# Splitting the FFN's layer norm between VectorE and ScalarE, moving the last image's ReLUs, and setting the times of all steps anew

## The chip, the cores and the metric

The kernel runs on one core of one Trainium2 chip. The metric is the device time in microseconds of one execution. Engines are called as in the profile: PE is TensorE's matmul, PEld its weight load, DVE is VectorE, ACT is ScalarE, POOL is GpSimd, SP is SyncE, which here only issues DMAs.

## The reference

Thirty-two images of 56 x 56 positions and 96 channels go through two layers.

```python
# layer 0: layer norm over channels, a product to 192 channels, a 3x3 convolution back to 96, silu, residual
h = (x - mu) * rsqrt(var + eps) * ln_w + ln_b
x1, z = split(einsum('bhwc,cd->bhwd', h, w_in) + b_in)
x = x + silu(conv3x3(x1, conv_w) + conv_b)
# layer 1, mixing: norm, product to 192, batch norm and relu, FFT over the 3136 positions,
# a diagonal complex product with relu on both parts, inverse FFT, product back to 96, batch norm
t = t + attn(_ln_t(t))
# layer 1, FFN: norm, product to 384 and relu, product back to 96;
# operands are rounded to an 8-bit float (5 exponent, 2 mantissa bits), sums to 16 bits
t = t + ffn(_ln_t(t))
```

`_ln_t` takes the mean and the variance over the 96 channels of a position and gives (t − mean) / sqrt(var + 1e-5). z is not used.

## The kernel before, in words

Each image passes four stages, which overlap with those of other images: at any time the convolution of one image, the first half of the mixing of the image before, the second half of the mixing of the one before that and the FFN of a still earlier one are under way. A tile of tokens has 112 partitions (positions) and 28 columns of positions; a group is four of these columns, so an image has 7 groups. The norm's statistics are taken in 4 chunks of two groups (the last has one).

The work is cut into steps. A step is a small Python function of one image, and `put(when, f, ...)` gives it a time; the unit is one eighth of an image's period, so steps of image b stand at 8 b + when. All steps of all images are sorted by these times and recorded in that order. A scheduler then sets the order of each engine's instructions from the recorded program by its own simulated times, so the order on an engine follows the times roughly, not exactly. Tiles come from pools in rotation. PSUM has four such rotations of two buffers each: "a" (the transposed tokens tp_n and the FFN's first product pf), "q" (im, cv, st of the convolution), "b" (pa, pg, pe, po) and "c" (ph, px, py).

The names that the text uses, in the order in which an image meets them:

- `fetch` (the DMA is issued in a helper, L356) loads a chunk xl of the image for the first norm, into one of three buffers; `take_in` takes its statistics (st_a, on DVE, L141; var_a, L145; rs_a = var to the power −1/2 on POOL, L147) and makes xa (DVE, L409). `make_image` multiplies xa on PE into im (L165), and ACT copies it into img (L167). `load` brings the same tokens a second time, into t, for the residual.
- `conv_part` is the convolution cv (L180, L184), three parts in each of three rounds; ACT and DVE make m, sd and s of it, `conv_tokens` turns s back into tokens st (PE, L216), and DVE adds them to t (L438).
- `norm_b` takes the statistics of the second norm (st_b, var_b, rs_b); `tokens_a` transposes a group into tp_n (PE, L158), and ACT copies it to n2t (L222). `forth` is the product ph (PE, L229), with a ReLU into h on ACT (L232); `forth_a` is the first transform pa (PE, L238), copied to u on ACT (L239); `store_a` writes u to da in HBM.
- `fetch_a` reads da back in another layout into at; `second` is the second transform px (PE, L253), from which ACT and DVE make av, sv and gt; `second_w2` is the product pg (PE, L296), gw its copy; `second_back` the first inverse transform pe (PE, L306), es its copy; `store_back` writes es to de in HBM.
- `fetch_y` reads de back into y, one of four buffers; `back` is the last inverse transform py (PE, L314); `back_end` adds it to t on DVE (L515) and takes the statistics of the FFN's norm (st_c, var_c, rs_c).
- `normal` (L520) makes the FFN's norm xn of a group in two calls of two columns each, all on DVE (L529); `ffn_start` transposes xn into tp_n (PE, L156) and copies it to n3t (ACT). `ffn_first` is pf (PE, L325) with the copy h1 on ACT (L327), three times per group; `ffn_middle` adds the bias and takes the ReLU into h2 and rounds it to hq (DVE, L335 and L336). In the last image two of the three ReLUs of a group are on ACT (L333). `ffn_second` is po (PE, L342), with the copy y1 on ACT (L346); `ffn_end` adds the bias and the residual (DVE, L351 and L352), and `store` writes the group of t to the result (`out`).

All loads and stores inside the loop are issued by SP, one queue in program order: one that has to wait holds up those behind it. `plan` (L558) holds the times of all steps; `CONV`, `FIRST`, `BACK` and `FFN` are the times at which the convolution, the first transform, the last transform and the FFN of an image begin, `S0` and `SS` the start and the spacing of the second transform's units. The last image and the two before it have corrections of their own.

Of the kernel before, what the change touches and what calls it, by code (L numbers as in the profile page):

```python
# [38 lines left out]
F32 = mybir.dt.float32  # L39
F16 = mybir.dt.float16  # L40
F8 = mybir.dt.float8e5
AF = mybir.ActivationFunctionType
ALU = mybir.AluOpType
AX = mybir.AxisListType

C = 96
HW = 56
N = HW * HW
N1, N2 = 112, 28
# [36 lines left out]
def hybrid_kernel(ctx: ExitStack, tc: tile.TileContext, x, par, spar, cpar, w_in, conv_w, w1, w2, fw1, fb1, fw2, fb2, fa, fb, ib, ia, rows6, out):  # L86
    nc = tc.nc
    nb = x.shape[0]
# [27 lines left out]
    b1q = const.tile([128, 3], F32, name="b1q")  # L116
# [13 lines left out]
    stp = ctx.enter_context(tc.tile_pool(name="stp", bufs=3))  # L130
# [198 lines left out]

    def ffn_relu(h1, hq, b, g, k):  # L330
        h2 = w3.tile([128, G4 * N1], F16, tag="h2", name=f"h2_{b}_{g}_{k}")
        if b == nb - 1 and k:
            nc.scalar.activation(h2, h1, AF.Relu, bias=b1q[:, k : k + 1])  # L333
        else:
            nc.vector.tensor_scalar(h2, h1, b1q[:, k : k + 1], 0.0, ALU.add, ALU.max)  # L335
        nc.vector.tensor_copy(hq[:, k, :], h2, saturate=False)  # L336

    def ffn_out(hq, b, g):
# [21 lines left out]
    class Image:  # L360


        def __init__(self, b):
            self.b = b
            self.tokens = x[b].rearrange("(p j) c -> p j c", j=N2)
            self.result = out[b].rearrange("(p j) c -> p j c", j=N2)
            self.t, self.s, self.n2t, self.hq = {}, {}, {}, {}
            self.u, self.at, self.gt, self.gw, self.held = {}, {}, {}, {}, {}
            self.xa, self.xc, self.rs, self.xl, self.y, self.norm = {}, {}, {}, {}, {}, {}

        def hold(self, half):
            n = G4 * (HALVES[half][1] - HALVES[half][0])
            self.t[half] = tpool.tile([N1, n, C + 1], F32, tag=f"t{half}", name=f"t_{self.b}_{half}")
# [146 lines left out]
    def normal(im, g, j):  # L520

        i = g // 2
        if j == 0:
            im.xc[g] = xnp.tile([N1, G4, C], F8, tag="xn", bufs=2, name=f"xn_{im.b}_{g}")
        mu, _, rs = im.norm[i]
        xc = im.xc[g]
        for j in (j, j + 1):
            at = g % 2 * G4 + j
            nc.vector.tensor_scalar(xc[:, j], im.chunk(i)[:, at, :C], mu[:, at : at + 1], rs[:, at : at + 1], ALU.subtract, ALU.mult, saturate=False)  # L529

    def ffn_start(im, g):
        im.held["n3", g] = ffn_tokens(im.xc.pop(g), im.b, g)
# [4 lines left out]
    def ffn_middle(im, g, k):  # L537
        if k == 0:
            im.hq[g] = w3.tile([128, 3, G4 * N1], F8, tag="hq", name=f"hq_{im.b}_{g}")
        ffn_relu(im.held.pop(("h1", g, k)), im.hq[g], im.b, g, k)  # L540
# [17 lines left out]
    def plan(b):  # L558
        im = Image(b)

        def put(when, f, *args):
            order.append((8 * b + when, len(order), lambda: f(im, *args)))

        last = b == nb - 1
        CONV, FIRST, BACK, FFN = ALL
        S0, SS = 0, 2
        if nb - 4 < b < nb - 1:
            BACK, FFN = BACK + 0.762, FFN + 0.3
        if last:

            FIRST, FFN = FIRST - 0.101, FFN - 0.127
            S0 = -0.975
        back_step, ffn_step = (0.763, 0.962) if last else (0.756, 0.962)

        for i, (j0, j1) in enumerate(LN_CHUNKS):
            at = CONV - 2.503 + 0.691 * i
            ahead = 12 if b == 0 else 2.55 - 0.221 * i
            put(CONV - 7.98 + 0.01 * i if b == 1 else at - ahead, fetch, i)
            put(at - 0.55, take_in, i)
            for j in range(0, j1 - j0, 2):  # L580
                put(at + 0.066 * j, make_image, i, j)
            put(CONV + 5.858 + 1.131 * i, norm_b, i)
            put(FIRST + 2 * i - 0.477, deviation, i)
            if b:
                put(CONV - 0.456 + 0.815 * i, load, i)
        put(CONV - 0.183, make_seam)
        for r in range(NR):
            at = CONV + 1.899 * r
            for part, when in enumerate((0, 0.321, 0.817)):
                put(at + when, conv_part, r, part)  # L590
            put(at + 0.72, conv_first, r)
            put(at + 1.356, conv_last, r)
            for half in range(2):
                put(at + 1.757 + 0.239 * half, conv_tokens, r, half)
                put(at + 1.818 + 0.239 * half, conv_end, r, half)
        for g in range(NG):
            at = FIRST + g
            put(at - 0.407, tokens_a, g)
            for j2 in range(2):
                put(at + 0.065 + 0.467 * j2, forth, g, j2)  # L600
                put(at + 0.536 + 0.58 * j2, forth_a, g, j2)
            put(at + 1.249, store_a, g)
            at = BACK + back_step * g
            put(max(S0 + 4 * SS - 0.003, at - 2.9), fetch_y, g)
            put(at, back, g)
            put(at + 0.06, back_end, g)
            at = FFN + ffn_step * g
            put(at - 0.797, normal, g, 0)
            put(at - 0.375, normal, g, 2)
            put(at - 0.365, ffn_start, g)  # L610
            for k in range(3):
                put(at + 0.336 * k, ffn_first, g, k)
                put(at + 0.336 * k + 0.208, ffn_middle, g, k)
            put(at + 0.912, ffn_second, g)
            put(at + 0.997, ffn_end, g)
            put(at + 1.5, store, g)
        for g in range(NS):
            put(max(FIRST + 7.508, S0 + g - (1.4 if g % 2 else 2.2)), fetch_a, g)
        for m, (p0, p1) in enumerate(UNITS):
            both = p1 - p0 > PG  # L620
            for at, u in ((0, 0), (0.606, 1), (1.069, 2)) if both else ((0, 0), (0.674, 2)):
                at += S0 + SS * m + (0.125 if m + u == 0 else 0)
                put(at, second, m, u)
                put(at + 0.22, second_parts, m, u)
                put(at + 0.512, second_relus, m, u)
            for j0 in range(0, (p1 - p0) // 2, 2):
                at = S0 + SS * m + (2.024 if both else 1.3) - 0.017 * j0
                put(at, second_w2, m, j0)
                put(at + 0.2, second_back, m, j0)
                put(at + 0.575, store_back, m, j0)  # L630
# [1 line left out]
    def load(im, i):  # L632
        im.load(i)

    CONV, FIRST, BACK, FFN = -14.872, -8.324, 8.016, 10.65
    ALL = CONV, FIRST, BACK, FFN
    for b in range(nb):
        plan(b)
# [15 lines left out]
    with tc.tile_pool(name="setup", bufs=1) as sp, tc.tile_pool(  # L654
        name="setup_ps", bufs=2, space=bass.MemoryType.PSUM
# [284 lines left out]
```

## Time and profile before

| | |
|---|---|
| time, three runs | 3091.17, 3093.26, 3093.85 us; median 3093.26 |
| the profiled execution | 3090.75 us |
| its span, from the first to the last instruction | 3089.0 us |
| mean granted TensorE clock | 0.986 |
| the clock in the last 96 us | 0.77 |
| PE, DVE, ACT busy from 1351 to 1448 us | 96.4, 79.2 and 69.6 of 97 us |
| DVE: one xn of 96 elements (x896) | 238.5 us together, 325 ns each |
| DVE: one ReLU of 448 elements (x658) | 213.9 us together, 330 ns each |
| ACT: one ReLU of 448 elements (x14) | 9.4 us together, 683 ns each |

A group's busy time counts overlapping instructions once, so it is below the count times the mean duration where they follow one another without a pause. Idle time that the page shows before an instruction belongs to its engine; what ended it is inferred from the semaphores.

### The profile page before, as it was taken

To read this page: it belongs to the slowest core of one execution; us is meant where nothing else is said; L and a number is where in the kernel's file an instruction comes from. 1 tells how busy PE (TensorE), PEld (TensorE's weight loads), DVE (VectorE), ACT (ScalarE), POOL (GpSimd) and SP (SyncE) were. 2 spreads that over 40 slices of the span, in tenths; PEclk is the share of its full clock that TensorE was granted. 3 is DMA by queue.
4 is the path that set the end of the run, shared out by engine and by line. 5 is a ranking of instruction groups with operands and counts; after the bars stand their busy time and mean duration, and the time that the engine had idled before them with its cause. 6 is when DMAs were issued, how large, how long until landed. Compare 5 with 4: busy or idle time off the path is not lost.

```text
span 3089.0 us, 84367 instructions
## 1 busy us (share of the span) xinstructions
PE 3000.8 (97%) x32693; PEld 2446.7 (79%) x32693; DVE 2439.2 (79%) x7554; ACT 2139.5 (69%) x5269; POOL 616.7 (20%) x398
## 2 busy tenths in 40 slices
PE   7899999999999999999999999999999999999998
PEld 5678788888788887788887888887888887788775
DVE  5548787888788888788888788888788887787778
ACT  3456667777667777677776677776677776676776
POOL 2202112222112222112221122221122221122111
PEclk9999999999999999999999999999999999999997
DMA  3532444443444443444443444444444444444442
GB/s 69 148 99 84 122 123 124 115 123 100 122 130 124 114 121 101 120 129 126 112 119 105 120 128 127 114 112 112 120 124 124 120 110 112 120 125 106 114 112 74
DMA packets 495436, 355.37 MB, mean 115 GB/s; under 512 B 329993, under 2 KB 459305, under 8 KB 494809
## 3 DMA queue, kind: packets, MB, share of 16 engines
q1 hardware_dynamic: 493146, 349.24, 42.8%
q8 instruction: 257, 4.21, 0.6%
q14 instruction: 145, 1.18, 0.1%
q10 hardware_dynamic: 1888, 0.74, 0.1%
HBM read 195.73 MB, written 154.14 MB: 113 GB/s over the span
## 4 chain that ended last, share of the span: by engine, by line
PE 88%; DMA 5%; DVE 3%; ACT 2%; issue 1%; SPq 0%; POOL 0%; DVEq 0%; ACTq 0%
PE cv L184 13%; PE ph L229 10%; PE px L253 10%; PE pa L238 9%; PE im L165 8%; PE pe L306 6%; PE pg L296 5%; PE py L314 5%; PE pg L292 5%; PE po L342 4%; PE pf L325 4%; PE cv L180 3%; PE st L216 3%; DMA de<-es 2%; PE tp_n L158 2%; DMA y<-de 2%
## 5 line engine op out<-in xcount | busy, mean ns | idle before, releaser
L184 PE MATMUL cv<-img,wv 97*32 97x196 f32 x13248 | 628.0, 332 | 0.0
L147 POOL TENSOR_TENSOR rs_c<-var_c,mhalf 112x8 f32<-112x8 f32 (+1 forms) x128 | 192.0, 1500 | 1965.0 <-DVE var_b L145 1261.4
L184 PEld LDWEIGHTS cv<-img,wv 97*32 97x32 f32 x13248 | 424.3, 109 | 112.6
L232 ACT ACTIVATE h<-ph,rs_b 112x192 f32<-112x192 f32 x896 | 338.3, 444 | 128.9 <-PE ph L229 127.9
L229 PE MATMUL ph<-w1a,n2t 97*112 97x192 f32 x1792 | 386.7, 338 | 3.3 <-DVE t L515 1.7
L253 PEld LDWEIGHTS px<-fb_sb,at 112*64 112x64 f32 (+1 forms) x3584 | 321.0, 167 | 75.9 <-issue 18.7
L238 PE MATMUL pa<-h,fa_sb 112*112 112x384 f32 x896 | 366.8, 491 | 4.9 <-DVE w1q L799 4.9
L327 ACT CAST h<-pf 128x448 f16<-128x448 f32 x672 | 364.8, 566 | 5.8 <-PE pf L325 3.0
L253 PE MATMUL px<-fb_sb,at 112*64 112x112 f32 (+3 forms) x3584 | 358.4, 274 | 7.4 <-DMA at<-da 3.8
L165 PE MATMUL im<-rows_sb,xa 112*97 112x168 f32 x1792 | 330.7, 310 | 3.1 <-DVE xa L409 1.9
L229 PEld LDWEIGHTS ph<-w1a,n2t 97*112 97x112 f32 x1792 | 273.2, 177 | 55.1 <-issue 15.9
L269 DVE SCALAR_TENSOR_TENSOR sv<-px,spar_sb,av 128x224 f32<-128x224 f32 (+2 forms) x352 | 153.9, 437 | 189.1 <-ACT av L260 188.3
L258 ACT ACTIVATE av<-px,spar_sb 128x224 f32<-128x224 f32 (+2 forms) x352 | 159.8, 454 | 200.5 <-PE px L253 199.6
L239 ACT COPY u<-pa 112x384 f32<-112x384 f32 x448 | 223.2, 498 | 102.9 <-PE pa L238 94.3
L165 PEld LDWEIGHTS im<-rows_sb,xa 112*97 112x97 f32 x1792 | 260.7, 166 | 38.5 <-issue 15.9
L147 POOL TENSOR_TENSOR rs_b<-var_b,mhalf 112x8 f32<-112x8 f32 (+1 forms) x128 | 201.8, 1578 | 425.8 <-DVE var_a L145 344.6
L336 DVE CAST hq<-h 128x448 fp8e5<-128x448 f16 x672 | 255.9, 387 | 10.2 <-ACT h L333 1.9
L335 DVE TENSOR_SCALAR h<-h,b1q 128x448 f16<-128x448 f16 x658 | 213.9, 330 | 58.9 <-ACT h L327 58.4
L141 DVE BATCH_NORM_STATS2 st_a<-xl 112x6 f32<-112x192 f32 x434 | 131.5, 353 | 154.6 <-DMA xl<-in_x 154.6
L296 PE MATMUL pg<-w2x,gt 128*112 128x96 f32 (+1 forms) x1792 | 243.5, 259 | 0.0
L529 DVE TENSOR_SCALAR xn<-t,st_c,rs_c 112x96 fp8e5<-112x96 f32 x896 | 238.5, 325 | 4.8 <-POOL rs_c L147 4.7
L296 PEld LDWEIGHTS pg<-w2x,gt 128*112 128x112 f32 (+1 forms) x1792 | 241.1, 178 | 0.0
(120 smaller groups left out, 6200.7 us busy)
## 6 DMA issues: line engine op xcount, KB each, us to landing
da<-u SPq DMA_DIRECT2D x224, 336.0 KB, 2.9
at<-da SPq DMA_DIRECT2D x224, 336.0 KB, 4.0
de<-es SPq DMA_DIRECT2D x448, 84.0 KB, 2.0
y<-de SPq DMA_DIRECT2D x224, 168.0 KB, 2.6
out<-t SPq DMA_DIRECT2D x224, 168.0 KB, 3.0
t<-in_x SPq DMA_DIRECT2D x96, 336.0 KB, 7.3
xl<-in_x SPq DMA_DIRECT2D x93, 336.0 KB, 4.1
t<-in_x SPq DMA_DIRECT2D x32, 168.0 KB, 4.3
```

The costliest lines, as they stand in the source:

```text
L147: nc.gpsimd.tensor_tensor(rs, var, mhalf[:, :n], ALU.pow)
L165: nc.tensor.matmul(ps[:, j], xa[:, j, :], rows6_sb, start=True, stop=True)
L184: tc.keep_in_program_order(nc.tensor.matmul(*args, start=(dx == 0), stop=(dx == 2)))
L229: nc.tensor.matmul(ph[:, j, :], n2t[:, 2 * j2 + j, :], w1a, start=True, stop=True)
L232: nc.scalar.activation(h[:, j], ph[:, j], AF.Relu, scale=rs[:, 2 * j2 + j : 2 * j2 + j + 1])
L238: nc.tensor.matmul(pa, fa_sb, h, start=True, stop=True)
L239: nc.scalar.copy(u[:, 2 * j2 : 2 * j2 + 2, :], pa)
L253: nc.tensor.matmul(px[rows, j], lhs, fb_sb[:, first(p) : first(p + 1)], start=True, stop=True)
L296: nc.tensor.matmul(pg[:, half, j, :], lhs, w2x, start=False, stop=True, skip_group_check=True)
L327: nc.scalar.copy(h1, pf)
L336: nc.vector.tensor_copy(hq[:, k, :], h2, saturate=False)
L529: nc.vector.tensor_scalar(xc[:, j], im.chunk(i)[:, at, :C], mu[:, at : at + 1], rs[:, at : at + 1], ALU.subtract, ALU.mult, saturate=False)
```

## The change

In `normal`, the first two columns of a group go to ACT, as an activation with the factor rs and the offset −mean · rs, and the last two stay on DVE. The offset, `shift`, is a new small tile, made on DVE once for each chunk. In `ffn_relu` the branch that put two of three ReLUs of the last image on ACT is gone. In `plan` nearly every time has another value, those of the last images too; no step is added or left out. In the diff below, steps of `plan` whose times are given only another value are cut where the text does not speak of them.

```diff
     def ffn_relu(h1, hq, b, g, k):
         h2 = w3.tile([128, G4 * N1], F16, tag="h2", name=f"h2_{b}_{g}_{k}")
-        if b == nb - 1 and k:
-            nc.scalar.activation(h2, h1, AF.Relu, bias=b1q[:, k : k + 1])
-        else:
-            nc.vector.tensor_scalar(h2, h1, b1q[:, k : k + 1], 0.0, ALU.add, ALU.max)
+        nc.vector.tensor_scalar(h2, h1, b1q[:, k : k + 1], 0.0, ALU.add, ALU.max)
         nc.vector.tensor_copy(hq[:, k, :], h2, saturate=False)
...
     def normal(im, g, j):
         i = g // 2
+        mu, _, rs = im.norm[i]
         if j == 0:
             im.xc[g] = xnp.tile([N1, G4, C], F8, tag="xn", bufs=2, name=f"xn_{im.b}_{g}")
-        mu, _, rs = im.norm[i]
+            if g % 2 == 0:
+                im.shift[i] = stp.tile([N1, mu.shape[1]], F32, tag="shift", name=f"shift_{im.b}_{i}")
+                nc.vector.scalar_tensor_tensor(im.shift[i], mu, -1.0, rs, ALU.mult, ALU.mult)
         xc = im.xc[g]
         for j in (j, j + 1):
             at = g % 2 * G4 + j
-            nc.vector.tensor_scalar(xc[:, j], im.chunk(i)[:, at, :C], mu[:, at : at + 1], rs[:, at : at + 1], ALU.subtract, ALU.mult, saturate=False)
+            t, scale = im.chunk(i)[:, at, :C], rs[:, at : at + 1]
+            if j < 2:
+                nc.scalar.activation(
+                    xc[:, j], t, AF.Identity, bias=im.shift[i][:, at : at + 1], scale=scale, saturate=False
+                )
+            else:
+                nc.vector.tensor_scalar(
+                    xc[:, j], t, mu[:, at : at + 1], scale, ALU.subtract, ALU.mult, saturate=False
+                )
...
         if nb - 4 < b < nb - 1:
-            BACK, FFN = BACK + 0.762, FFN + 0.3
+            BACK, FFN = BACK + 0.4, FFN + 0.284
         if last:
-            FIRST, FFN = FIRST - 0.101, FFN - 0.127
-            S0 = -0.975
-        back_step, ffn_step = (0.763, 0.962) if last else (0.756, 0.962)
+            CONV, FIRST, FFN = CONV - 0.074, FIRST - 0.016, FFN - 0.721
+            S0, SS = -0.831, 2.033
+        back_step, ffn_step = (0.82, 0.962) if last else (0.775, 0.971)
         for i, (j0, j1) in enumerate(LN_CHUNKS):
-            at = CONV - 2.503 + 0.691 * i
-            ahead = 12 if b == 0 else 2.55 - 0.221 * i
+            at = CONV - 2.485 + 0.531 * i
+            ahead = 12 if b == 0 else 2.489 - 0.221 * i
             put(CONV - 7.98 + 0.01 * i if b == 1 else at - ahead, fetch, i)
             put(at - 0.55, take_in, i)
...
             at = FFN + ffn_step * g
             put(at - 0.797, normal, g, 0)
-            put(at - 0.375, normal, g, 2)
-            put(at - 0.365, ffn_start, g)
+            put(at - 0.639, normal, g, 2)
+            put(at - 0.329, ffn_start, g)
...
-            put(at + 0.912, ffn_second, g)
-            put(at + 0.997, ffn_end, g)
-            put(at + 1.5, store, g)
+            put(at + 0.96, ffn_second, g)
+            put(at + 0.986, ffn_end, g)
+            put(at + 1.483, store, g)
         for g in range(NS):
-            put(max(FIRST + 7.508, S0 + g - (1.4 if g % 2 else 2.2)), fetch_a, g)
+            put(max(FIRST + 7.433, S0 + g - (1.479 if g % 2 else 1.667)), fetch_a, g)
...
-    CONV, FIRST, BACK, FFN = -14.872, -8.324, 8.016, 10.65
+    CONV, FIRST, BACK, FFN = -15.042, -8.232, 8.036, 10.805
```

More of the change, by code (lines that the diff above doesn't have):

```diff
@@ L369, in __init__ @@
             self.xa, self.xc, self.rs, self.xl, self.y, self.norm = {}, {}, {}, {}, {}, {}
+            self.shift = {}
         def hold(self, half):
@@ L580, in plan @@
             for j in range(0, j1 - j0, 2):
-                put(at + 0.066 * j, make_image, i, j)
-            put(CONV + 5.858 + 1.131 * i, norm_b, i)
+                put(at + 0.08 * j, make_image, i, j)
+            put(CONV + 5.967 + 1.132 * i, norm_b, i)
             put(FIRST + 2 * i - 0.477, deviation, i)
             if b:
-                put(CONV - 0.456 + 0.815 * i, load, i)
-        put(CONV - 0.183, make_seam)
+                put(CONV - 0.346 + 0.78 * i, load, i)
+        put(CONV - 0.078, make_seam)
         for r in range(NR):
-            at = CONV + 1.899 * r
-            for part, when in enumerate((0, 0.321, 0.817)):
+            at = CONV + 1.91 * r
+            for part, when in enumerate((0, 0.139, 0.817)):
                 put(at + when, conv_part, r, part)
             put(at + 0.72, conv_first, r)
-            put(at + 1.356, conv_last, r)
+            put(at + 1.385, conv_last, r)
             for half in range(2):
-                put(at + 1.757 + 0.239 * half, conv_tokens, r, half)
-                put(at + 1.818 + 0.239 * half, conv_end, r, half)
+                put(at + 1.757 + 0.21 * half, conv_tokens, r, half)
+                put(at + 1.858 + 0.21 * half, conv_end, r, half)
         for g in range(NG):
@@ L600, in plan @@
                 put(at + 0.065 + 0.467 * j2, forth, g, j2)
-                put(at + 0.536 + 0.58 * j2, forth_a, g, j2)
-            put(at + 1.249, store_a, g)
+                put(at + 0.536 + 0.659 * j2, forth_a, g, j2)
+            put(at + 1.2, store_a, g)
             at = BACK + back_step * g
-            put(max(S0 + 4 * SS - 0.003, at - 2.9), fetch_y, g)
+            put(max(S0 + 3 * SS + 2 - 0.003, at - 3.004), fetch_y, g)
             put(at, back, g)
-            put(at + 0.06, back_end, g)
+            put(at + 0.113, back_end, g)
             at = FFN + ffn_step * g
             put(at - 0.797, normal, g, 0)
-            put(at - 0.375, normal, g, 2)
-            put(at - 0.365, ffn_start, g)
+            put(at - 0.639, normal, g, 2)
+            put(at - 0.329, ffn_start, g)
             for k in range(3):
@@ L613, in plan @@
                 put(at + 0.336 * k + 0.208, ffn_middle, g, k)
-            put(at + 0.912, ffn_second, g)
-            put(at + 0.997, ffn_end, g)
-            put(at + 1.5, store, g)
+            put(at + 0.96, ffn_second, g)
+            put(at + 0.986, ffn_end, g)
+            put(at + 1.483, store, g)
         for g in range(NS):
-            put(max(FIRST + 7.508, S0 + g - (1.4 if g % 2 else 2.2)), fetch_a, g)
+            put(max(FIRST + 7.433, S0 + g - (1.479 if g % 2 else 1.667)), fetch_a, g)
         for m, (p0, p1) in enumerate(UNITS):
             both = p1 - p0 > PG
-            for at, u in ((0, 0), (0.606, 1), (1.069, 2)) if both else ((0, 0), (0.674, 2)):
+            for at, u in ((0, 0), (0.606, 1), (1.099, 2)) if both else ((0.028, 0), (0.674, 2)):
                 at += S0 + SS * m + (0.125 if m + u == 0 else 0)
@@ L624, in plan @@
                 put(at + 0.22, second_parts, m, u)
-                put(at + 0.512, second_relus, m, u)
+                put(at + 0.47, second_relus, m, u)
             for j0 in range(0, (p1 - p0) // 2, 2):
-                at = S0 + SS * m + (2.024 if both else 1.3) - 0.017 * j0
+                at = S0 + SS * m + (2.024 if both else 1.221) - 0.01 * j0
                 put(at, second_w2, m, j0)
```

## The prediction

> **What bounds the kernel now.** First the page: the span and the busy shares.
>
> ```profile
> span 3089.0 us, 84367 instructions
> PE 3000.8 (97%) x32693; PEld 2446.7 (79%) x32693; DVE 2439.2 (79%) x7554; ACT 2139.5 (69%) x5269; POOL 616.7 (20%) x398
> PE 88%; DMA 5%; DVE 3%; ACT 2%; issue 1%; SPq 0%; POOL 0%; DVEq 0%; ACTq 0%
> ```
>
> TensorE sets the time: 88% of the chain that ended last is its own work. Moving work between VectorE (79%) and ScalarE (69%) gains nothing by itself; only 88 us in which PE has no matmul can be won. The windows by image put some 32 of these before 290 us, 25 after 2895 us, and about 30 in between: a little over 1 us per image. Second, the waits of that middle stretch (300 to 2835 us; columns: total us, times, longest):
>
> ```profile
> DVE st_a L141 <- DMA xl<-in_x: 141.2, 54, 5.0
> PE py L314 <- DMA y<-de: 15.9, 18, 2.0
> PE tp_n L158 <- ACT h L327: 10.7, 27, 0.6
> ```
>
> So two waits make up nearly all of it. Third, the timeline of PE at the turn of an image:
>
> ```profile
> 1528.06 0.35 PE L325 MATMUL pf<-n3t,w1q 96*128 96x448 fp8e5 x1
> 1528.26 0.55 PE L158 MATMUL tp_n<-ident,t 112*97 112x112 f32 x4
> 1529.19 0.62 PE L158 MATMUL tp_n<-ident,t 112*97 112x112 f32 x4 [0.39 <-ACT h L327]
> ...
> 1536.53 0.90 PE L314 MATMUL py<-y,ia_sb 113*112 113x384 f32 x2 [0.59 <-DMA y<-de]
> ```
>
> The second tp_n takes the PSUM buffer of the pf 1.1 us ahead of it, which ScalarE has yet to empty. It starts 0.93 us after the first, where an unhindered one is followed after 0.38 us: 0.55 us lost. The py stands behind the convolution and waits for its load. The convolution's last group to py takes 2.60 us; the same pair with y there takes 1.94 us later in this timeline: 0.66 us lost for 0.59 us idle. Why y is late, VectorE and the SP queue say:
>
> ```profile
> 1529.65 1.17 DVE L141 BATCH_NORM_STATS2 st_a<-xl 112x6 f32<-112x192 f32 x4 [3.56 <-DMA xl<-in_x]
> 1531.71 0.35 DVE L351 TENSOR_TENSOR y<-y,b2q 112x384 f16<-112x384 f16 x1
> 1532.28 0.56 DVE L352 TENSOR_TENSOR t<-t,y 112x384 f32<-112x384 f32 x1
> ```
>
> ```profile
> 1518.39 0.44 SPq L356 DMA_DIRECT2D xl<-in_x  x1
> ...
> 1521.18 2.25 SPq L469 DMA_DIRECT2D at<-da  x3
> 1523.52 0.38 SPq L356 DMA_DIRECT2D xl<-in_x  x1
> ...
> 1532.86 0.32 SPq L549 DMA_DIRECT2D out<-t  x1
> 1533.68 1.27 SPq L506 DMA_DIRECT2D y<-de  x3
> ```
>
> The third chunk's load (xl, 1523.52) is queued behind three loads of at and lets VectorE stand 3.56 us. Behind st_a on VectorE stand the last ReLUs and sums of group 5; the store `out` waits for that sum (1532.84); the y loads stand behind this store on SP; PE gets y 2.6 us after issue.
>
> **What the skill says.** "TensorE: Matmul & The Clock Gate", in the section on the array's 32×32 parts: ScalarE and VectorE are strict FIFOs, only PE pulls weight loads forward. The 3.56 us above agree: ready ReLUs stood behind st_a. "ScalarE: Activation LUTs", What ACT_TABLE_LOAD costs: 186 ns + 0.833 ns per element + 93 ns per pointer operand. For 112 elements and two pointers 465 ns; the trace has 438 (av, L259). Same page, Rules for kernel authors: ReLU belongs on VectorE. The trace agrees: 683 ns (L333) against 330 (L335). "Perfetto Trace Analysis", Identifying the Most-Contended Engine: matmul busy is no measure of headroom, gaps on the engine that should be full are what to trace back; done above.
>
> **The change, part by part.**
>
> *Norm (normal, L520).* Per image 14 of 28 VectorE instructions leave: 238.5/896 = 0.27 us each without overlap, 3.7 us. Four `shift` products come: the nearest row is var (112x8, 171 ns), 0.7 us. VectorE has 3.0 us less per image. ScalarE gets 14 activations of 96 elements with two pointers: 438 − 16 × 0.833 = 425 ns, about 0.31 behind one another (L259 at 224 elements follows itself after 0.42), so 4.4 to 6.0 us per image; it goes from 68.5 to at most 74.5 of 93 us. Cover: PE's own work. The new wait is ScalarE for shift, behind GpSimd's rs_c (1.65 us). Queued behind it are the h activations that pa waits for. In the program's new order the shortest ph-to-pa stretch on PE is 2.4 us (1.6 before), and two h need about 0.75: 1.6 us to spare. Bounds: nothing, to the rival below. I take 1 us per image at most, within "new waits".
>
> *Last image's ReLUs.* ScalarE loses 9.4 us (L333, all of it), VectorE gains 14 × 0.33 = 4.6. With its norm (−3.7 + 0.7) VectorE has 1.6 us more in the last image, where it was busy 31.2 of 36 us (3050 to 3086). Against that, in its last 12 us VectorE waited 1.9 us for those ReLUs. Image 30's norm takes 3 us off VectorE in the stretch from 3010 to 3050, where it was 92 to 100% busy; PE gaps there end on VectorE only in part. Together I take −1.5 us; bounds −6 to +5 (all of both gains, or the added VectorE work and reordered steps in full).
>
> *Times.* Nothing is computed that was not: the matmuls are as many, 1616 SP rows stay. GpSimd keeps its order but for the four-wide powers, one place earlier. What moves in the order of each engine, per image (distances on PE are counted in the built program's order, each group at the spacing from its start to the next one's in the timeline: a px or ph pair 0.65 to 0.9 us, an im pair 0.57, a po 0.61, a pf 0.20, a convolution part 1.9):
> - tp_n of group 3 leaves the pf of group 6 and stands behind the convolution's first three parts, py 0 and a px: 8 us later, its buffer long empty. Nearest such pair in the new order: 1.6 us apart, against 0.45. Gain 27 × 0.55 = 14.9 us.
> - On SP the third xl load goes right behind the second, ahead of the three at loads, which then wait a few us. They don't mind: 18.7 us of matmuls lie between the last pa and the first px, for 0.3 + 2.9 (da) + 4.0 (at). xl now waits for its buffer, that is for xa, 1520.2 in this timeline: issue near 1520.3 instead of 1523.5. The second load took 4.0 us, the third 6.1 in a crowd, so it lands between 1524.3 and 1526.4, and st_a ends by 1527.5, 3.3 us earlier. po of group 5 moves 1.0 us later on PE, so the sum then waits for po: end about 1531.1, out 1531.2, y 1532.0, landed by 1534.9. py is due at 1535.9: 1 us to spare. Gain up to 15.9 × 0.66/0.59 = 17.8; I take 15, for transfers that are late at times (the longest wait was 2.0).
> - The other PSUM turns and copies have 0.6 us or more on ScalarE in the new order by the same counting, hq to po 3.6 us (1.7 before), cv to its transposition 2.7 (2.3). pg to pe falls from 2.9 to 1.9, es to py from 12.0 to 10.4, tp_n of group 0 to ph from 2.4 to 1.5 with 0.85 needed. For new waits I add 3 us; bounds 0 to 15 (0.5 per image).
> - The start keeps its order on PE but for a few places: 0, bounds ±3.
>
> Sum against the profiled run's own 3090.75 us (span 3089.0): −14.9 − 15 + 3 − 1.5 = −28.4, so 3062.3. The median of the runs shown is 2.5 us above that run: **3065**.
>
> **Rivals.** *Only the PSUM wait goes:* two xl loads together are slower, VectorE still stands, out and y are as late as before. −14.9 + 3 − 1.5: 3080. For it: the chain has four links with 1 us to spare. Against: the at loads no longer go ahead. *Nothing shows:* the wait at one place moves to the next (pg to pe, or tp_n to ph) and the ends shuffle: 3087 to 3099. Against: PE had only these two regular gaps. *Slower, ScalarE stuck behind rs_c:* if shift comes more than 1.6 us after ScalarE reaches the norm, h is late for pa. At 1 us lost for one of an image's four pairs, 32 us: 3125. For it: the four norms stand together ahead of h; GpSimd's powers queue. Against: VectorE stood at the same place for only 4.7 us in all waiting for rs_c.
>
> **Numbers.** No change is 3087 to 3099 (0.2%, about what a measurement of this kernel can tell). Both waits gone 0.62 (3054 to 3075), one gone 0.20 (3076 to 3088), nothing 0.07, slower 0.11. The low end is 17.8 + 14.9 + 6 off 3093; the high end takes in the second case and the edge of the third. Faster 0.80, same 0.09, slower 0.11.
>
> **What would show it.** Right: "PE tp_n <- ACT h" and "PE py <- DMA y" near nothing in the middle, st_a's wait on xl under 90 us, images 92.2 us apart instead of 92.7 to 94.3. Wrong: py still waits (a late xl), or ScalarE shows a wait on DVE shift with PE pa waiting for h.

## The result and the profile after

The changed kernel takes 3053.97 us (median of 3049.28, 3053.87, 3054.07 and 3059.97) against 3092.22 (four runs): a ratio of 0.988, with a 95% interval from 0.9861 to 0.9898. The forecast was 3065, so the sign was right and the gain, 38 us, larger than the 28 of the sum; the time lies at the low edge of the range that the text gave for both waits gone, 3054 to 3075. The profiled execution is the slowest of the four, 3059.97. A second profile of the same kernel, taken later (the run "after again" below), is of a run of 3052.15; both are used.

First the page after: span, busy time of PE, DVE and ACT, and the chain that ended last, by engine.

```profile
span 3058.2 us, 84433 instructions
PE 2982.3 (98%) x32693; PEld 2439.2 (80%) x32693; DVE 2347.6 (77%) x7248; ACT 2276.6 (74%) x5703; POOL 647.1 (21%) x398
PE 74%; DVE 11%; DMA 8%; ACT 4%; issue 2%; POOL 1%; SPq 0%; POOLq 0%; ACTq 0%; DVEq 0%
```

PE's busy time fell by 18.5 us though the matmuls are the same. Some 9.5 of them fell in the 24 images of the table below, where the clock is full but for 3 us: a busy stretch of PE contains short stalls that the page doesn't list as idle. Another 8.1 fell behind the last convolution's start, where the granted clock differs (see below). VectorE fell by 91.6 us, ScalarE rose by 137.1. PE's share of the chain differs from profile to profile: it is 84% in the second one.

Then the waits between 300 and 2835 us (total us, times, longest):

```profile
DVE st_a L141 <- DMA xl<-in_x: 46.6, 29, 3.0
ACT xn L532 <- DVE shift L526: 17.1, 27, 0.6
PE py L314 <- DMA y<-de: 11.9, 19, 1.9
```

("In the middle" stands below for this stretch, or for 300 to 2800 us, or, where it is said, for the 24 images of the table.) tp_n's wait for ScalarE is gone, VectorE's wait for xl fell by two thirds, ScalarE has the new wait for shift once per image. But py still waits for y.

The timeline of PE at the turn of the same image (its convolution starts at 1431.36):

```profile
1430.89 0.55 PE L158 MATMUL tp_n<-ident,t 112*97 112x112 f32 x4
...
1438.41 0.90 PE L314 MATMUL py<-y,ia_sb 113*112 113x384 f32 x2 [0.87 <-DMA y<-de]
1439.15 1.04 PE L253 MATMUL px<-fb_sb,at 112*128 112x114 f32 x8
1440.03 0.55 PE L158 MATMUL tp_n<-ident,t 112*97 112x112 f32 x4
```

The second tp_n stands behind py and px, as the prediction had it from the program's order, and no longer waits. py is late again.

Where the time came from, by the start of each image's convolution in the traces (us):

| stretch | before | after | after again |
|---|---|---|---|
| start to the convolution of image 4 (the first is 0) | 318.5 | 323.6 | 321.9 |
| from there to image 28 (24 images) | 2233.8 | 2211.6 | 2205.0 |
| image 28 to 31 | 282.0 | 275.4 | 274.9 |
| last convolution's start to the end | 254.7 | 247.5 | 248.5 |

In the 24 images the convolutions start 91.9 us apart by the median, 91.7 in the second profile, against 92.85 before.

The last row is not what it seems. The page gives the TensorE clock that was granted, in tenths of full speed, for 40 slices of the span; first before, then after:

```profile
PEclk9999999999999999999999999999999999999997
PEclk8999999999999999999999999999999999999998
```

In the traces the clock falls to half for stretches of 3 to 26 us, and there a py starts 640 ns after the one ahead of it, in place of 325. From the last convolution's start to the end PE was busy at half clock for 42 us before, 24 after and 26 in the second profile. Half of that time is at most what the lower clock costs: 21, 12 and 13 us, an estimate. Without it the last row would be 233.7, 235.4 and 235.6, so the lower clock of before would cover all of the 7.2 and 6.2 us. Whether the change brings the higher clock or chance does is not shown. In the 24 images PE was at half clock for 3.4 us in the first profile of the changed kernel and never in the other two.

Whole runs point the same way. On the chip of "after again" 35 runs of the kernel before have mean clocks from 0.983 to 0.991, and a straight line through them gives 2.6 us less for 0.001 more. The changed kernel's five runs there have a median clock of 0.988 against 0.986, which is worth some 5 of the 34 us between them, by estimate.

Both kernels run the same matmuls, so PE's start-to-start times, summed by kind of group, say what the 24 images gained. Inside the tp_n groups, a usual hand-over set aside where two of them no longer follow each other: −15.4 us (−15.7 again). At py, by what it starts later behind the convolution than one whose y is there: 14.5 us before, 12.8 after, 8.2 again. The remaining 5.1 (6.8) us are spread over the hand-overs from one group to the next, of which an image has 148 in place of 151. The middle, then, is where the change is seen to gain.

### The profile page after: what moved, and what is told of

Its sections match the earlier page's. It is cut to its first block, busy times and chain, and to the rows that moved or that the text cites. A ratio compares the mean times of both kernels' runs of the same rounds, so it can differ in the third digit from the quotient of the medians.

```text
span 3058.2 us, 84433 instructions
## 1 busy us (share of the span) xinstructions
PE 2982.3 (98%) x32693; PEld 2439.2 (80%) x32693; DVE 2347.6 (77%) x7248; ACT 2276.6 (74%) x5703; POOL 647.1 (21%) x398
## 3 DMA queue, kind: packets, MB, share of 16 engines
q8 instruction: 257, 4.21, 0.6%
## 4 chain that ended last, share of the span: by engine, by line
PE 74%; DVE 11%; DMA 8%; ACT 4%; issue 2%; POOL 1%; SPq 0%; POOLq 0%; ACTq 0%; DVEq 0%
PE cv L184 12%; PE ph L229 9%; PE px L253 9%; PE pa L238 8%; PE im L165 5%; PE py L314 5%; PE pe L306 5%; PE pg L296 4%; PE pg L292 4%; DMA de<-es 3%; PE po L339 3%; PE cv L180 3%; PE pf L325 3%; PE st L216 2%; DMA xl<-in_x 2%; PE tp_n L158 2%
## 5 line engine op out<-in xcount | busy, mean ns | idle before, releaser
L147 POOL TENSOR_TENSOR rs_c<-var_c,mhalf 112x8 f32<-112x8 f32 (+1 forms) x128 | 208.9, 1632 | 1906.2 <-DVE var_c L145 882.9
L229 PE MATMUL ph<-w1a,n2t 97*112 97x192 f32 x1792 | 379.1, 334 | 1.5 <-DVE sv L272 0.7
L165 PE MATMUL im<-rows_sb,xa 112*97 112x168 f32 x1792 | 319.8, 311 | 3.1 <-DVE t L436 1.3
L147 POOL TENSOR_TENSOR rs_b<-var_b,mhalf 112x8 f32<-112x8 f32 (+1 forms) x128 | 226.9, 1781 | 429.1 <-DVE var_a L145 387.8
L167 ACT COPY img<-im 97x336 f32<-97x336 f32 x448 | 205.8, 461 | 53.4 <-PE im L165 30.6
L436 DVE TENSOR_TENSOR t<-st,t 112x512 f32<-112x512 f32 (+1 forms) x192 | 118.6, 618 | 157.4 <-PE st L216 123.4
```

What stands on the lines that cost most here:

```text
L147: nc.gpsimd.tensor_tensor(rs, var, mhalf[:, :n], ALU.pow)
L165: nc.tensor.matmul(ps[:, j], xa[:, j, :], rows6_sb, start=True, stop=True)
L229: nc.tensor.matmul(ph[:, j, :], n2t[:, 2 * j2 + j, :], w1a, start=True, stop=True)
```

## The experiments

**1. The two halves of the change alone.** `e1_split_only` is the kernel before with the new `normal`:

```diff
-            nc.vector.tensor_scalar(xc[:, j], im.chunk(i)[:, at, :C], mu[:, at : at + 1], rs[:, at : at + 1], ALU.subtract, ALU.mult, saturate=False)
+            t, scale = im.chunk(i)[:, at, :C], rs[:, at : at + 1]
+            if j < 2:
+                nc.scalar.activation(xc[:, j], t, AF.Identity, bias=im.shift[i][:, at : at + 1], scale=scale, saturate=False)
+            else:
+                nc.vector.tensor_scalar(xc[:, j], t, mu[:, at : at + 1], scale, ALU.subtract, ALU.mult, saturate=False)
```

> The kernel before with the new norm alone (two of four chunks on ScalarE, shift on VectorE), old step times, old ReLUs. With it the planner puts tp_n of group 3 behind the convolution's first three parts, py and px, as in the changed kernel; PE has 10.4 us of work between the last pe and py 0 (11.0 before, 9.5 in the changed kernel). Theory (PE's gaps set the time): the wait of tp_n on ScalarE is gone, 27 x 0.55 = 15 us, and py waits about as before: 3072 to 3080. Rival (the step times make the gain): 3087 to 3099. Rival (the split makes all of it): 3050 to 3060.

`e2_times_only` has the new `plan` with the old `normal` and `ffn_relu`:

> The changed kernel with the old norm (all on VectorE) and the old ReLUs: the new step times alone. The planner then puts py 0 ahead of the convolution's third part; PE has 9.3 us of work between the last pe and py 0. Theory (PE's gaps): tp_n's wait is gone (-15 us), py waits about 0.2 us per image longer than in the changed kernel (0.44 there): 3068 to 3085. Rival (the split makes the gain): 3087 to 3099. Rival (the times make all of it): 3050 to 3060.

Measured: the split alone 3181.14 us, 1.0304 times before (1.0276 to 1.0331); the times alone 3112.2, 1.009 (1.0058 to 1.0123). No theory had either: both halves lose, by 93 and 24 us, and together they gain 38. The waits of the split alone, 300 to 2800 us:

```profile
PE ph L229 <- ACT h L232: 25.5, 26, 1.0
PE tp_n L158 <- ACT h L327: 23.1, 26, 1.7
ACT xn L535 <- DVE shift L529: 17.6, 29, 0.8
```

This tp_n is another than the prediction's: one that follows a pf and a ph later in the image. The first line is the prediction's slow rival in another form: h is late there too, but what waits is not pa but the next ph, for the PSUM buffer that h empties. Timelines of PE and of ScalarE at the place:

```profile
1497.82 0.90 PE L229 MATMUL ph<-w1a,n2t 97*112 97x192 f32 x4
...
1500.62 0.91 PE L229 MATMUL ph<-w1a,n2t 97*112 97x192 f32 x4 [0.98 <-ACT h L232]
```

```profile
1498.41 1.54 ACT L535 ACTIVATE xn<-t,shift,rs_c 112x96 fp8e5<-112x96 f32 x4 [0.62 <-DVE shift L529]
1499.86 0.71 ACT L232 ACTIVATE h<-ph,rs_b 112x192 f32<-112x192 f32 x2
```

ScalarE waits 0.62 us for shift, makes four norms in 1.54 us and only then the h whose end frees a buffer for the second ph. Between the two ph PE has a py and a tp_n to do. The changed kernel has the same four norms ahead of the same h, but its new times put a pa and a po there too (lines of "after again"):

```profile
1447.34 0.81 PE L238 MATMUL pa<-h,fa_sb 112*112 112x384 f32 x2
1447.99 0.78 PE L339 MATMUL po<-w2q,hq 128*112 128x96 fp8e5 x12
...
1449.51 0.74 PE L229 MATMUL ph<-w1a,n2t 97*112 97x192 f32 x3
```

ScalarE's h ends there at 1449.46, PE starts the next ph at 1449.51: the place fits with nothing to spare. So the split needs the new times, though this place is only 25.5 of the 84.6 us that the 24 images lose. Why the times need the split is not settled to one wait. With the norm back on VectorE the scheduler takes another order: PE leaves the convolution eight times per image in place of seven, py stands ahead of its third part, and PE's start-to-start times over 24 images, each put down to the matmul that begins it, grow at pf (by 11 us against before), po (10; PE waits 8.8 us for VectorE's hq in the middle), pa (7), im (6) and px (5), which eats the 16 that tp_n gives.

**2. Is it that place?** `e9_split_odd`, the split alone with two norms in the burst in place of four:

```diff
-            if j < 2:
+            if j < 2 and g % 2:
```

> The split alone with the old step times, but only the odd groups have two chunks on ScalarE (the even groups stay on VectorE): at the place where four norms stand on ScalarE between two h there are now two, some 0.75 us less. PE's order at that place is unchanged (ph, py, tp_n, ph). Theory (the burst of norms ahead of h holds PE's ph): the wait of ph on ScalarE's h falls from 25.5 us in the middle to under 8, and the time from 3181 to 3120 to 3165. Rival (ScalarE is late everywhere, since the new work is in no place it has room): the waits on ScalarE fall by about half in all places. Rival (another cause): 3175 to 3185.

Measured: 3179.71 us (1.0284, 1.0261 to 1.0306). PE's wait of ph on ScalarE's h is gone from the list, as the first theory said of the place, but the time is not: PE now waits 58.3 us, 16 times and up to 5.5 us, for VectorE's hq ahead of po. The time falls where the last rival, another cause, had it. The place is shown; its price in the whole is not: PE has another order in every second image, and the clock fell too. PE was at half clock for 75 us of the 24 images, and its four runs have mean clocks of 0.975 to 0.977 against 0.984 to 0.989 for the kernel before on that chip.

`e10_three_on_act`, the changed kernel with `if j < 3`:

> The changed kernel with three of four chunks of the norm on ScalarE in place of two; the order on PE in the middle stays. In the changed kernel ScalarE ends the h behind the four norms 0.15 us before PE needs its buffer for the next ph; six norms last 0.7 us longer. Theory (room at this one place decides): PE's ph waits 0.4 to 0.7 us per image for ScalarE's h, 3063 to 3072. Rival (ScalarE's total counts, it would be at 77 to 80%): within 4 us of the changed kernel's 3052.

Measured: 3207.08 us (1.0366, 1.0334 to 1.0398), some 150 us worse than the changed kernel, ten times what was expected of the place. Waits, 300 to 2800 us:

```profile
ACT xn L532 <- DVE shift L526: 38.0, 38, 1.9
PE py L314 <- DMA y<-de: 33.1, 23, 3.3
PE im L165 <- ACT img L167: 15.9, 12, 1.3
```

ph's own wait on h is 7.4 us in 13 places. At one wait of im, ScalarE works without a pause from before three norms (1479.14) until the img copy that PE waits for (1484.37), so what the norms take there is not made up for ahead of that copy. How the 150 us divide over the places is not settled: PE's order alternates between two from image to image, and PE was at half clock for 58 us of the 24 images, against 3 in the changed kernel.

**3. Who makes y late.** `e3_xl_pinned` is the kernel before, with the third xl load kept in the program's order:

```diff
-            in_turn(im.xl[i], im.tokens[:, j0:j1, :], im.b < 3)
+            in_turn(im.xl[i], im.tokens[:, j0:j1, :], im.b < 3 or i == 2)
```

> The kernel before with one edit: the third xl load keeps the order of the program on SP, so that it stands ahead of the at loads. The planner then also moves tp_n of group 3 behind px and leaves 8.9 us of PE work between the last pe and py 0 (11.0 before). Theory A, as predicted (late xl, VectorE, out, y is the chain that makes py wait): st_a's wait on xl under 60 us and py's wait gone, 15 + 15 us gained: 3060 to 3066. Theory B (py waits for the spectrum's way through DRAM: last pe, ScalarE's es, store of de, load of y, some 10 us): tp_n gains 15, py loses about 1 us per image against 0.6: 3082 to 3092, with py's wait on y about 27 us in the middle.

Measured: 3113.02 us (1.0082, 1.0054 to 1.0111).

```profile
DVE st_a L141 <- DMA xl<-in_x: 36.0, 27, 2.9
PE py L314 <- DMA y<-de: 27.7, 23, 3.2
```

Theory A falls: VectorE's wait for xl went from 141 to 36 us, and py waits more, not less. (That alone would not decide, since PE's order moved too and py is due earlier, as expected; the table below shows that `out` left 3.2 us earlier than before and y only 0.55.) Theory B's 27 us is met. The total is 20 us above its upper end; half of the images have another order, in which PE waits for s ahead of st (12.1 us), which nothing had foreseen. The chain can be followed in the traces, as medians over 25 images, in us from the convolution's first matmul (DMAs by the start of their issue):

| kernel | pe starts | es copied | last store of de issued | out issued | y issued | py starts |
|---|---|---|---|---|---|---|
| before | −6.33 | −5.51 | −0.40 | 2.83 | 3.66 | 6.48 |
| after | −4.20 | −3.38 | −0.27 | 1.42 | 3.86 | 6.49 |
| de from ScalarE's queue | −4.21 | −3.38 | −2.98 | 1.42 | 1.85 | 6.12 |
| pf from another ring | −5.98 | −5.16 | −0.11 | 3.14 | 4.01 | 6.96 |
| third xl load ahead | −4.11 | −3.33 | 0.05 | −0.35 | 3.11 | 6.27 |

After the change `out` leaves 1.4 us earlier, as predicted, and y doesn't follow: it now waits for the last store of de to land. From the start of that store's issue to the start of y's pass 4.1 us by the median before and 4.2 after. SP at this place in the changed kernel:

```profile
1429.75 0.93 SPq L353 DMA_DIRECT2D t<-in_x  x2
1430.78 1.01 SPq L498 DMA_DIRECT2D de<-es  x2
1431.88 1.22 SPq L558 DMA_DIRECT2D out<-t  x2
1435.46 4.19 SPq L504 DMA_DIRECT2D y<-de  x5
```

es was copied by 1427.98. Its stores leave 2.8 us later, behind two loads of t, which wait for an older `out` store to land (124 us of SP's waits in the middle, 44 before); the second store needs 3.6 us from the end of its issue until y may go.

`e4_de_on_act`, the changed kernel with these two stores on ScalarE's queue:

```diff
-            nc.sync.dma_start(rows[:, half, j0 : j0 + 2], es[:, half])
+            (nc.scalar if m == 3 else nc.sync).dma_start(rows[:, half, j0 : j0 + 2], es[:, half])
```

> The changed kernel with the two stores of the last unit's es (L498, m == 3) issued on ScalarE's queue, so that they don't stand on SP behind two loads of t that wait for an older out store; PE's order stays. Theory B (de's landing releases y): de goes out 2 us earlier, y is released by out at 1.4 us after the convolution's start in place of 4.0, py's wait in the middle falls from 11.9 to under 3 us: 3042 to 3048. Rival (y is held by out or its own buffers just after): 3050 to 3056. Rival (ScalarE's issue of stores delays its copies): 3057 to 3070.

Measured: 3051.09 us (0.9877, 0.9846 to 0.9907). ScalarE's and SP's timelines one image later, and the wait in the middle:

```profile
1510.45 0.48 ACT L308 COPY es<-pe 112x384 f32<-112x384 f32 x1
1510.96 0.31 ACTq L498 DMA_DIRECT2D de<-es  x1
```

```profile
1513.63 2.73 SPq L558 DMA_DIRECT2D out<-t  x2
1516.47 5.27 SPq L504 DMA_DIRECT2D y<-de  x5
```

```profile
PE py L314 <- DMA y<-de: 0.7, 2, 0.4
```

The time is not the 3042 to 3048 of theory B, but the mechanism is as it says: y leaves 2.0 us earlier, py waits no more, the 24 images take 2200.2 us (11.4 and 4.8 less than in the two profiles of the changed kernel), 91.64 us each by the median. But the stretch from the last convolution's start to the end grew to 251.6.

`e7_after_again` and `e8_de_on_act_head` put it on one chip; the second keeps SP for the last three images and takes the old spacing of `take_in` and `make_image` in the first three:

> The changed kernel once more, on the same chip as the next one: 3049 to 3060, 1.1 to 1.3% under before; py's wait on y in the middle 8 to 14 us.

> The changed kernel with the last unit's es stored from ScalarE's queue in all but the last three images, and with the old spacing of chunks and image products in the first three images. Theory: py's wait in the middle goes as in the run with these stores on ScalarE (-11 us against the changed kernel), the fourth image's convolution starts 3 to 5 us earlier than in the changed kernel, the tail is the changed kernel's: 12 to 16 us faster than the changed kernel on the same chip. Rival (the start is set by the weights' loads, not by these times): 9 to 12 us faster. Rival (the gain in the middle is given back in the tail): within 4 us of it.

Measured: 3052.18 us (0.9892, 0.9872 to 0.9912) and 3054.15 (0.9898, 0.9877 to 0.992). The 24 images gain 4.1 us (py's wait 7.0, a little under what was expected, to 2.1), the start loses 1.0 and the end 2.6: by the numbers the rival "given back in the tail". But PE does not wait longer in that tail: its idle time fell from 27.3 to 25.7 us and its busy time rose from 221.3 to 225.3, at a mean clock of 0.904 against 0.929. So matmuls at a lower clock made it longer, not a wait; why the clock was lower is open. No kernel tried here is measurably faster than the changed one.

**4. What tp_n's wait is worth.** `e5_y1_on_dve` was to bring ScalarE earlier to the pf whose buffer tp_n takes, by moving one copy off it:

```diff
-        nc.scalar.copy(y1, po)
+        (nc.vector.tensor_copy if g == 5 else nc.scalar.copy)(y1, po)
```

> The kernel before with one edit: the copy y1<-po of group 5 on VectorE instead of ScalarE, 0.43 to 0.49 us ahead of ScalarE's copy of the pf whose PSUM buffer the late tp_n takes. PE's order is the one of before but for the last image. Theory (that PSUM wait costs PE 0.55 us per image): ScalarE comes to the pf 0.45 us earlier, tp_n's wait in the middle falls from 10.7 to under 3 us, PE gains 9 to 13 us; VectorE holds y1 behind st_a, so that sum, out and y are up to 0.5 us later, which costs 0 to 10 us: in all 0 to 13 us faster than before, and the time from one convolution to the next shows both. Rival (PE's wait there is filled by later stalls): tp_n's wait falls and the time between images stays within 0.1 us of before's 92.85.

Measured: 3088.92 us (1.0005, 0.9992 to 1.0018), tp_n's wait 10.2 us as before. A miss of the design: the time that the copy leaves on ScalarE can't be used there.

```profile
1524.90 0.44 ACT L167 COPY img<-im 97x336 f32<-97x336 f32 x1 [0.44 <-PE im L165]
1525.24 0.54 ACT L327 CAST h<-pf 128x448 f16<-128x448 f32 x1
```

With y1 gone, it idles 0.44 us for the last im, copies that, and then pf: the wait is set by the order of these two copies, not by the load.

`e12_pf_other_ring` takes the cause away instead, in the kernel before:

```diff
-        pf = psum.tile([128, G4 * N1], F32, tag="a", bufs=2, name=f"pf_{b}_{g}_{k}")
+        pf = (psq if g == 6 and k == 2 else psum).tile([128, G4 * N1], F32, tag="q" if g == 6 and k == 2 else "a", bufs=2, name=f"pf_{b}_{g}_{k}")
```

> The kernel before with one edit: the last pf of each image (group 6, k = 2) takes its PSUM buffer from the ring of im, cv and st instead of that of tp_n and pf. The second tp_n then takes a buffer that ScalarE emptied long before; pf and the first tp_n change places on PE, all else stays in its order up to the last images. Theory (the two waits stand in series): tp_n's wait goes from 10.7 to under 2 us in the middle, the convolution starts 0.55 us earlier after the last pe, but y is released as late as before, so that py's wait grows from 15.9 to 25 to 31 us: 0 to 6 us faster than before. Rival (the waits are independent, as the prediction's sum had them): py's wait stays near 16 us, 12 to 16 us faster, images 92.3 us apart in place of 92.85.

Measured: 3097.39 us (1.003, 1.0016 to 1.0043), slower by a little. Over the 24 images PE's time inside tp_n falls by 14.4 us, about the predicted price; at py it grows by 5.8, at the convolution's start by 6.3, and with 1.1 us gained elsewhere 3.4 remain. Start and end took 9.5 us more than in the profile of before. The slower total fits the clock: the 15 runs have a median clock of 0.983, the 20 of before on that chip 0.9865, worth some 9 us at 2.6 us for 0.001, by estimate. So only the 24 images speak of the waits. Waits, 300 to 2800 us:

```profile
PE py L314 <- DMA y<-de: 22.6, 24, 2.5
PE cv L180 <- ACT img L417: 5.1, 25, 0.2
```

There the waits stand in series. PE comes to the convolution earlier and finds ScalarE still copying the image, then comes to py earlier and finds y no earlier. The expectation had y, not the image.

**5. The last image's ReLUs.** `e6_relus_only` is the kernel before with them on VectorE, `e11_after_old_relus` the changed kernel with the old `ffn_relu`:

```diff
-        if b == nb - 1 and k:
-            nc.scalar.activation(h2, h1, AF.Relu, bias=b1q[:, k : k + 1])
-        else:
-            nc.vector.tensor_scalar(h2, h1, b1q[:, k : k + 1], 0.0, ALU.add, ALU.max)
+        nc.vector.tensor_scalar(h2, h1, b1q[:, k : k + 1], 0.0, ALU.add, ALU.max)
```

> The kernel before with the last image's ReLUs on VectorE and nothing else; every engine's order is the same up to the last image. Theory (part of the gain in the tail is theirs): ScalarE is relieved of 9.4 us, the stretch after the last convolution's start goes from 254.7 to 249 to 253 us, the time down by 2 to 6 us. Rival (the tail's gain of 7 us comes from new step times and the norm): the stretch stays within 2 us or grows by up to 5 us, as VectorE takes 4.6 us more at a place where it was busy.

> The changed kernel with the last image's ReLUs of k > 0 on ScalarE again; every engine's order is the same up to there. Theory (with the new step times the ReLUs on VectorE pay): 2 to 6 us slower than the changed kernel, the stretch after the last convolution's start 250 to 254 in place of 248. Rival (the times and the norm make the tail's gain): within 2 us of it.

Measured: 3088.74 us (1.0005, 0.9994 to 1.0016) and 3065.1 (0.9921, 0.9902 to 0.994). With the old times the ReLUs give nothing, the last stretch is 256.9 us against 254.7. In the changed kernel it is 252.6 without the new ReLUs against 248.5 in "after again"; the ratios, 0.9921 and 0.9892, are of different comparisons and differ by about the width of their intervals. The clock is not the same here either. The last stretch in all these profiles, with an estimate of the clock's price, half of the time that PE was busy at half clock:

| kernel | us | mean clock | PE busy at half clock | without the clock's price |
|---|---|---|---|---|
| before | 254.7 | 0.900 | 42.0 | 233.7 |
| before with the new ReLUs | 256.9 | 0.894 | 44.6 | 234.6 |
| after | 247.5 | 0.936 | 24.2 | 235.4 |
| after again | 248.5 | 0.929 | 25.8 | 235.6 |
| after with the old ReLUs | 252.6 | 0.907 | 33.5 | 235.8 |
| after with de from ScalarE's queue | 251.6 | 0.913 | 35.6 | 233.8 |
| the same, but not in the last three images | 251.1 | 0.904 | 39.2 | 231.5 |

The last column moves by 4 us in all, and by 0.2 between the two kinds of ReLU in the changed kernel. So neither the ReLUs nor the change is shown to shorten the tail.

## Why the prediction was right or wrong, point by point

- **What bounds the kernel: right.** PE does, and what was won in the 24 images is stalls of PE. The moves of work are of the predicted size (VectorE −91.6 us against −91.4 from the text's terms; ScalarE +137.1, within the 131 to 183 that they give). One xn on ScalarE takes 484 ns, not the estimated 425. The text's 68.5 us of ScalarE per image are those of its windows of 96.5 us; per image of 93 us it was 66.3, and is 70.9 after.
- **tp_n's PSUM wait, −14.9: right in place and size, wrong as a term that stands alone.** It fell by 15.4 us over 24 images. With little else moved ("pf from another ring") only 3.4 of 14.4 us are left in the time of these images.
- **y, −15: wrong.** From 24 images 1.7 us came in one profile and 6.3 in the other. The step that failed is "out 1531.2, y 1532.0". The first half held: `out` leaves 1.42 us after the convolution's start, where the text had 1.5. But y also needs de, whose last store leaves SP late and takes 3.6 us to land. The text had the shortest es-to-py stretch on PE fall "from 12.0 to 10.4" and put no price on the way through HBM inside it. The trace of before showed it, in the same image, in a line of the SP queue that the prediction does not show:

```profile
1527.67 2.40 SPq L500 DMA_DIRECT2D de<-es  x2
1532.86 0.32 SPq L549 DMA_DIRECT2D out<-t  x1
1533.68 1.27 SPq L506 DMA_DIRECT2D y<-de  x3
```

The second of these stores starts at 1529.73, and y leaves 3.95 us later. Where `out` left earlier, in the changed kernel, that stretch is 4.2 us by the median, so an earlier `out` alone had next to nothing to give.

- **New waits, +3: smaller.** In the middle PE shows 0.5 us of them. ScalarE's wait for shift is there, 0.6 us per image, and hidden, as costed. But "1.6 us to spare" was counted for h on its way to pa. The next ph, for which h frees a buffer, was not counted, and there next to nothing is spare: 0.05 us in "after again", and less than nothing in the split alone.
- **The tail, −1.5: not shown.** It was −7.2 and −6.2, but the difference in the clock would cover all of it (table above). The sum has no term for the clock, though before's own trace had 0.77 in the last 96 us.
- **The start, 0 ± 3: outside its bound, but not clear of noise.** +5.1 and +3.4. Profiles of kernels that start in the order of before (`e5_y1_on_dve`, `e6_relus_only`, `e12_pf_other_ring`) gave 315.8, 321.3 and 324.6 where its own gave 318.5, so all of this may be chance.
- **What the sum left out:** the 5 to 7 us at hand-overs between PE's groups, which show in no line of waits, and the clock, which would cover the 6 to 7 us of the last stretch. (Images 28 to 31 gave 6.6 and 7.1 us; the two waits at their predicted size are 3.3 of them, and some 3 may be chance, since `e5_y1_on_dve` and `e6_relus_only` took 278.3 and 278.9 us there where before took 282.0.) Hand-overs and clock made up for y, so the forecast was better than its parts, and that is luck.
- **The signs to look for:** tp_n's wait gone and st_a's under 90 us came true (46.6), images 92.2 us apart was met by the mean of the 24 images (92.15, and 91.9 in the second profile). py's wait near nothing did not come, and "a late xl" was the wrong reason for it.
- **The slow rival** did not decide this change. With the old times its kind is real: in the split alone PE waits 25.5 us for an h behind the four norms. But shift holds ScalarE there for 0.62 us, not the 1.6 of the text, and the wait is of ph, not of pa.

## What to carry to other kernels

Before the end of a wait is counted as a gain, follow the engine to its next two or three waits, and for each ask by what it is released and how much later: only about the smallest of these margins is gained (here 3.4 of 14.4 us). A load goes when the last of all the things that it waits for is done, so price a store's way to memory and back beside the queue that the load stands in. Work moved to a less busy engine needs room at the place where it stands in that engine's queue; its busy share doesn't tell, and step times set for one division of work can lose with another. Compare the granted clock stretch by stretch before a difference is put down to the program.

## What the hardware showed beside that

PE pays for leaving the convolution. Its matmuls start in fours: the four within some 20 ns, the next four 147 ns after the fourth, so that four of 196 columns take 166 ns together, about what one matmul of ph with 192 columns takes (162). But the first ph or px behind the last of them starts 258 ns after it (257 to 260 in all 107 such places of the middle of before), where a ph follows an st after about 110 ns. Against the 147 ns of going on that is some 0.11 us each time, seven times per image, and no line of waits shows it.

The stores of 84 KB land 2.0 us after their issue by the median, but y could go only some 3.6 us after the last of them at the place that matters here, among loads of 336 KB.
